# One written-out order of 5935 steps replaced by another in a two-layer graph kernel

## The chip, the cores and the metric

The kernel runs on one core of one Trainium2 chip. The metric is the device time of one execution in microseconds (us). The engines are named as in the profile: PE (TensorE; its weight loads are PEld), DVE (VectorE), ACT (ScalarE), POOL (GpSimd) and SP (SyncE, which here only issues DMAs). Each engine works through its own instructions in program order, and waits at an instruction until what that instruction needs is there.

## The reference, cut to what matters

`x` is 32 batches of 512 channels by 1024 nodes, `adj` is 512 by 512, all in float32.

```
h   = relu(layernorm(x))                        # layer 0, over the 1024 nodes
q   = wq . h ;  k = wk . h                      # one number per node
att = softmax over n of leaky_relu(q[n] + k[m], 0.01)
agg[c, m] = sum over n of h[c, n] * att[m, n]
x   = x + relu(adj @ agg + bm)
h   = relu(layernorm(x))                        # layer 1
x   = x + (adj*adj).T @ h + bias
```

The 1024 x 1024 attention matrix is never formed. A score is linear in `q[n]` on either side of `q[n] + k[m] = 0`, so each output row needs two running sums over the nodes sorted by `q`. The kernel sorts by counting, takes running sums over the sorted rows of `v = adj @ h`, and looks up, for every node, the row of the table where its sign changes.

## The kernel before, in words

`ORDER` (line 35) is one long text, and it is the whole schedule. `names` holds 226 lanes, one for each kind of step and index (`value` 0 to 7, `scan` 0 to 8, and so on); a lane holds that step for each batch in turn. Two base-36 digits give `ahead * 226 + lane`: take from that lane the step that stands `ahead` places from its front (lines 757 to 763). The steps are then issued in that order under `tc.manual_schedule()`, so the text fixes the order of the instructions on every engine and of the DMAs on every queue, and the order in which tiles are taken from the pools.

The steps of a batch, in the order in which they depend on each other:

- `load` (SP, 512 KB each, four), `stats0`, `norm0`, `slopes0`, `relu0` make `h` of layer 0 in place. `stats0` is DVE work for the first six batches and ACT work after.
- `scores` (PE) and a copy on ACT make `q` and `k`; `row` and `columns` bring them into rows and columns; `rank` (DVE, eight) counts each node's place among the `q`; `lower` (ACT, eight) counts the place at which its sign changes; `factors`, `to_rows` and `from_rows` make indices and exponents of them.
- `value` (PE, eight, 8 matmul records each, L474) makes `v` in a PSUM bank, `spread` (ACT, L481) copies it out, `scatter` (POOL, an indirect DMA, L487) writes its rows to a table in DRAM in sorted order.
- `fetch` (SP, three DMAs of 792 KB, L503) reads the table back, `weights` (ACT), `later` (DVE), `totals` (PE) and `stationary` (POOL, L546) make the weights.
- `scan` 0 to 8 (PE, L562; number 4 is L559) makes running sums of 128 rows at a time, one half upwards and one half downwards. Each `scan` has two matmuls, one for each half, and each half needs the last row of the half before it. This carried row is written into the next `vs` rows by `sums`: for batches 5 to 27 ACT copies the sums out (L574), then SP copies one row of 2 KB for each half (L576, L577); for the other batches ACT copies the two rows itself (L572, L573). `sums` then writes the running sums to the table by two DMAs of 132 KB on SP (L580, L581).
- `gather` (POOL, eight indirect DMAs, L586) looks up three table rows for each node, `excess` and `divide` make three factors, `weigh` (ACT, L611) and `combine` (DVE, L615, sixteen) add the rows up. There is one `g` buffer, so the gathers of a batch follow the last `turn` of the batch before.
- `turn0` and `turn1` (PE, L622) transpose the result into a bank; DVE adds it onto `x`, which `reload` (SP, four of 512 KB) has brought again (L626).
- `means`, `stats1` (ACT, four), `norm1`, `slopes1`, `relu1` make `h` of layer 1; `seed` (ACT, L648), `mix` (DVE, L644), `propagate` (PE, 14, L657) and `finish` (DVE, L670 and L674) multiply by `adj*adj` in seven block products instead of eight for batches 0 to 27; the last four batches use `sow`, `plain` (PE, eight, L689) and `close`, with eight. `store` (SP, four of 512 KB, L701) writes the batch out.

There are 8 PSUM banks for all of this, 16 row buffers for `x`, `h` and `mx`, and 5 buffers of three table blocks each for `vs`. Steps of several batches lie between each other: around the scans of batch 14 stand the values of batch 16, the statistics of batch 12 and the products of batch 11. In the order before, the steps from batch 9 to batch 21 repeat: each stretch from a batch's first `scan` to the next batch's is the same 187 steps, shifted by one batch. Before and after that the stretches differ.

Of the kernel before, what the change touches and what calls it, by code (L numbers as in the profile page):

```python
# [33 lines left out]
0a0405002u2w2y30942y01022u96342w352y3630372u30329a332y343a03393b2w382i0y362j2k160w0d090b080c351014  # L34
340m0h0r0u36180n0l0p370o0v120g0q320t330z0k130s3a060f391117353b380e0x192l1i1b0y0j1530942y1c2z371a0i
0w321d331j1e163a2i341g3610071f39353b1h2m2j2k140u18380v120m0h0z132n0r2l110l0n170p0g0o0x0k190q0t0f0y
2w2o2y2x0s2p2u0e3u153v2q1k1i1c0w0j1t1a2m1b1l1d100i161u34141j1h1m18362i3w351f0u371v1g371e3232332j1n
12333a2k0v341w36393b1o0z131x0h0m2l1p112n0l1y0r0g1q170n0x0k1z0f0p1r192v0o310e2w2o30202p1i1c2q0q1s0j
3u150t1a1k0i383v1t0y1b350s1j1e3a371l1g212m162i1f0w1h1u1d39221m2j142k3b25101v3w2338291n1832260u331w
270h0m283a1o242l0v0l1x0z0r0g120n0k130p1p17110f0o2n1y0e0q1q1i1a190y0t0j1z1c2r0i1b0s1r160x2s1j1h2a2d  # L40
562b5c2g1f572i581g5b0w5i551e2e5h2h5e2o5j2c2p2k102f3u592j155k1d205g5a145d1s185f392m2q1k3v3m3r3s0m3q
3o1t3p3t0u210r3b0h1l0n0v121u2l0l0p1m130o3n0z3w1v0g220q252t380k1n230t11290f1w26273e0e1o28170x3g0j24
1x0i3f1p190y3h1j1e2n1y1i1c3c0s3d1q1g3l2m2i1a0w1b1z1f3i1h1r154t3j2k101d2r3k4u2y2s4w2a4v2d41552b5b3z
2g58452e4g3y5h2u2h5d442c4i2f5a16475f3x4m145i40434k185g5k422o314f5e2j462p204n3u562q1k4x4y1s4p1t4950
3v57591l4h5j5148215c4z0h4a1u4b4r4o0l4c522v2x4j1m2w4q2z3m3p1v3w3t3q3r4d1n3n3s1w3o4e22251o4s0u231x2t
4l290g3e26543h1p2l53270v282n0k1y243f0f1q123g0z0e1z0j3c341r3d110i3l3i1j1e360x4t1i1c3j1g3k4u4w303541
1a4v2y4g42131b2r3z2s0m454n3y0r444i171f0n472u4m191h0p4k3x0o43400q464f151d310t4x4y2o4z49202p503u4p2q
0s1s4h2a2m1k51373v4856214a4r322d332b5c4b1t4o574c583a4j395b2v1l2z4q3b2w554d522x1u4e4l381m2g4s532e5i
542i5e3w5d0y5h1v2h1n2j5j2c165k2k2f0w591w5g5a5f1o143m1x3p3o3s3t0m3q1p0r3r3n2n1y1022240n0h280p1q2718
2t0u0l3e261z292l231r0g3g250v123f0k3h0z0f133c0o3d0q0e3l113i1i1c340j1a0x4t3j1b0i3k364u41304v2z4w2x1j  # L50
1g422y2o4g3z2p20451e4n2r3u3y2q3x1s4i402s43171f1935463v4f1h21444p0t4x4y151d1k4m0s50484z2a2m37492d4r
47324h2b332g4a1t563a4k5c4b394o573b2u584c51524j385b1l2e5i2v2h314q2i5e5j2w5k4e555d1u2c2k0y4s2f592j5g
545a5f4d5h161m4l533m3r1v3w3s0m3t3q3p0r3o3n0w220n250p231n0h142910261w2t0l3e273g282l0u240g3f183h1o0k
0v1x3c123d0o0f3l0z3i0e130q4t3j1i1c1p0j3k112n1a1y344u1b4v4w0i413z36452r4g1j1g17423y2s19351h4i444n1f
0x3x4m0t1e400s432a302m2y151d2v2d462b2g4f2u2o5h1q2e2p2h474x3u2c4y1z4z2f2q1k50374p495f5d4855324h331r
4r3a5a4a395i5b204b5g1t4o3b584c5k384j5e4d4q562x571s31592z1l5j52213v5c4e4l1u4k2i4s0y542w51532j1m162k
3m1v3w3p3r3s3o3t3n3q0w22250m230r1n0h29140n10262t1w0l0p273e282l0u240g3g183f1o0k0v1x3h0f123c0o0z3d13
0q0e3l1i1c3i1p0j34111a2n4t1b0i1y3j0x3k2r4u1j1g364w4v1e2s413z303y2z171f44194g351h454m3x420t4i2y4043
0s4n151d2m2f462c2h2u472o4f2e2p2g4x3u1q2b4y2d2q371k504p495h5f1z485d322a4h334a4r3a55395a4b4o3b5i521r
5b384j4c5g20581t5k2i4q5e560y57595j2v5c314k2x2j1s164z512w1l213v2k3m1u3r3p3s3t3q3o4d0m4e0r3n0n0w220p  # L60
250h231m1429102t0l1v3w3e263g4s270g540u183f284l243h0k533c1n0o3d0v120f1w3l3i2l0z0e130q4t3j1i1c113k4u
0j341a1b4w1o174v36410i424g1x1j1f3z3y0x2r4n192s351h1g1p3x300t2y1e452v2x1y0s444i402m151d2a432d2n374m
464f5c56472b324x2g4y2e4z492h502c4p2f4k4a4h33511q572u3a4o48395e5j1z5k4b3b4r58384c5b4j522o5i314d2w4q
2p553u2q2z1r4l591k535a204e5d1t5h5g2i4s5f0y541s162j1l213v2k3m1u3r3s3p3t3q3o3n0w0m22250r230n1m0h2914
100p3w2t1v0l263e273g2l0u280g3f24183h1n0k0v123c1w3d0o0f3l0z3i0e130q4t3j1i1c1o0j3k111a1x344u1b4v4w0i
413z3y361p2r4g441j1g2n1y2s1745191h4m35421f4i3x1e0x0t4n400s2a2m432d302y151d2b462g4f2e5c2h47572c2v4x
2f4y4p49504z4k482o2x4h2p51561q3u374r2q1k5e5j4a1z5k32584b334o3a2u5b4c31394j525i3b551r2w4q2z384d595a
205d1t4e4l5h5g2i4s5f0y54532j1s161l213v2k3m1u3r3s3p3t3q3o3n0m0w220r250n231m0h14290p103w1v2t0l3e263g
272l0u280g3f24183h1n0k0v123c1w3d0o0f3l0z3i0e130q4t3j1i1c1o0j3k111a1x344u1b4v4w0i413z3y361p2r4g441j
1g2n1y2s1745191h4m35421f4i3x1e0x0t4n400s2a2m432d302y151d2b462g4f2e5c2h47572c2v4x2f4y4p49504z4k482o  # L70
2x4h2p51561q3u374r2q1k5e5j4a1z5k32584b334o3a2u5b4c31394j525i3b551r2w4q2z384d595a205d1t4e4l5h5g2i4s
5f0y54532j1s161l213v2k3m1u3r3s3p3t3q3o3n0m0w220r250n231m0h14290p103w1v2t0l3e263g272l0u280g3f24183h
1n0k0v123c1w3d0o0f3l0z3i0e130q4t3j1i1c1o0j3k111a1x344u1b4v4w0i413z3y361p2r4g441j1g2n1y2s1745191h4m
35421f4i3x1e0x0t4n400s2a2m432d302y151d2b462g4f2e5c2h47572c2v4x2f4y4p49504z4k482o2x4h2p51561q3u374r
2q1k5e5j4a1z5k32584b334o3a2u5b4c31394j525i3b551r2w4q2z384d595a205d1t4e4l5h5g2i4s5f0y54532j1s161l21
3v2k3m1u3r3s3p3t3q3o3n0m0w220r250n231m0h14290p103w1v2t0l3e263g272l0u280g3f24183h1n0k0v123c1w3d0o0f
3l0z3i0e130q4t3j1i1c1o0j3k111a1x344u1b4v4w0i413z3y361p2r4g441j1g2n1y2s1745191h4m35421f4i3x1e0x0t4n
400s2a2m432d302y151d2b462g4f2e5c2h47572c2v4x2f4y4p49504z4k482o2x4h2p51561q3u374r2q1k5e5j4a1z5k3258
4b334o3a2u5b4c31394j525i3b551r2w4q2z384d595a205d1t4e4l5h5g2i4s5f0y54532j1s161l213v2k3m1u3r3s3p3t3q
3o3n0m0w220r250n231m0h14290p103w1v2t0l3e263g272l0u280g3f24183h1n0k0v123c1w3d0o0f3l0z3i0e130q4t3j1i  # L80
1c1o0j3k111a1x344u1b4v4w0i413z3y361p2r4g441j1g2n1y2s1745191h4m35421f4i3x1e0x0t4n400s2a2m432d302y15
1d2b462g4f2e5c2h47572c2v4x2f4y4p49504z4k482o2x4h2p51561q3u374r2q1k5e5j4a1z5k32584b334o3a2u5b4c3139
4j525i3b551r2w4q2z384d595a205d1t4e4l5h5g2i4s5f0y54532j1s161l213v2k3m1u3r3s3p3t3q3o3n0m0w220r250n23
1m0h14290p103w1v2t0l3e263g272l0u280g3f24183h1n0k0v123c1w3d0o0f3l0z3i0e130q4t3j1i1c1o0j3k111a1x344u
1b4v4w0i413z3y361p2r4g441j1g2n1y2s1745191h4m35421f4i3x1e0x0t4n400s2a2m432d302y151d2b462g4f2e5c2h47
572c2v4x2f4y4p49504z4k482o2x4h2p51561q3u374r2q1k5e5j4a1z5k32584b334o3a2u5b4c31394j525i3b551r2w4q2z
384d595a205d1t4e4l5h5g2i4s5f0y54532j1s161l213v2k3m1u3r3s3p3t3q3o3n0m0w220r250n231m0h14290p103w1v2t
0l3e263g272l0u280g3f24183h1n0k0v123c1w3d0o0f3l0z3i0e130q4t3j1i1c1o0j3k111a1x344u1b4v4w0i413z3y361p
2r4g441j1g2n1y2s1745191h4m35421f4i3x1e0x0t4n400s2a2m432d302y151d2b462g4f2e5c2h47572c2v4x2f4y4p4950
4z4k482o2x4h2p51561q3u374r2q1k5e5j4a1z5k32584b334o3a2u5b4c31394j525i3b551r2w4q2z384d595a205d1t4e4l  # L90
5h5g2i4s5f0y54532j1s161l213v2k3m1u3r3s3p3t3q3o3n0m0w220r250n231m0h14290p103w1v2t0l3e263g272l0u280g
3f24183h1n0k0v123c1w3d0o0f3l0z3i0e130q4t3j1i1c1o0j3k111a1x344u1b4v4w0i413z3y361p2r4g441j1g2n1y2s17
45191h4m35421f4i3x1e0x0t4n400s2a2m432d302y151d2b462g4f2e5c2h47572c2v4x2f4y4p49504z4k482o2x4h2p5156
1q3u374r2q1k5e5j4a1z5k32584b334o3a2u5b4c31394j525i3b551r2w4q2z384d595a205d1t4e4l5h5g2i4s5f0y54532j
1s161l213v2k3m1u3r3s3p3t3q3o3n0m0w220r250n231m0h14290p103w1v2t0l3e263g272l0u280g3f24183h1n0k0v123c
1w3d0o0f3l0z3i0e130q4t3j1i1c1o0j3k111a1x344u1b4v4w0i413z3y361p2r4g441j1g2n1y2s1745191h4m35421f4i3x
1e0x0t4n400s2a2m432d302y151d2b462g4f2e5c2h47572c2v4x2f4y4p49504z4k482o2x4h2p51561q3u374r2q1k5e5j4a
1z5k32584b334o3a2u5b4c31394j525i3b551r2w4q2z384d595a205d1t4e4l5h5g2i4s5f0y54532j1s161l213v2k3m1u3r
3s3p3t3q3o3n0m0w220r250n231m0h14290p103w1v2t0l3e263g272l0u280g3f24183h1n0k0v123c1w3d0o0f3l0z3i0e13
0q4t3j1i1c1o0j3k111a1x344u1b4v4w0i413z3y361p2r4g441j1g2n1y2s1745191h4m35421f4i3x1e0x0t4n400s2a2m43  # L100
2d302y151d2b462g4f2e5c2h47572c2v4x2f4y4p49504z4k482o2x4h2p51561q3u374r2q1k5e5j4a1z5k32584b334o3a2u
5b4c31394j525i3b551r2w4q2z384d595a205d1t4e4l5h5g2i4s5f0y54532j1s161l213v2k3m1u3r3s3p3t3q3o3n0m0w22
0r250n231m0h14290p103w1v2t0l3e263g272l0u280g3f24183h1n0k0v123c1w3d0o0f3l0z3i0e130q4t3j1i1c1o0j3k11
# [690 lines left out]
```

## Time and profile before

| | |
|---|---|
| runs, us | 2300.36, 2294.92, 2301.21 (median 2300.36) |
| profiled execution, us | 2299.28 |
| its span, us | 2297.6 |
| mean granted TensorE clock | 0.992 |
| PE busy | 2225.3 us (97%) |
| DVE, ACT, POOL busy | 1735.6 (76%), 1703.1 (74%), 704.9 (31%) |
| DMA over the span | 657.77 MB, mean 286 GB/s |

The span is from the first to the last instruction; the 1.7 us between it and the execution's own time lie around it. The page's second part cuts the span into 40 slices of 57 us. A table by windows gives the busy time of each engine in chosen stretches; what a window has over PE's busy time is time in which PE had nothing in work. A matmul that waits for its data behind one that is in work can show as a longer busy time of its line, so a wait can also hide in a busy PE: a line of the timeline then takes longer than the same line elsewhere.

### The profile page before, as it was taken

What the parts mean: (1) busy time and instruction counts of PE and PEld (TensorE: products, weight loads), DVE (VectorE), ACT (ScalarE), POOL (GpSimd) and SP (SyncE); (2) the same over time, 40 slices, a digit from 0 to 9 for tenths busy, and PEclk for the clock granted to TensorE, in tenths of its full rate; (3) what the DMA queues carried; (4) which work ended last, traced back from release to release, by engine and by line L of the source; (5) the groups of instructions that cost most, each with busy time, mean ns of one, the idle gap of its engine ahead of it and who ended that gap; (6) DMA issues with size and microseconds to landing.
All of it is one profiled execution on the core that took longest, in us unless ns stands there. A gap on an engine that the chain in (4) does not pass through costs nothing. (4 is left out here: it accounts for less than half of the span.)

```text
span 2297.6 us, 28803 instructions
## 1 busy us (share of the span) xinstructions
PE 2225.3 (97%) x7344; PEld 954.0 (42%) x7344; DVE 1735.6 (76%) x4876; ACT 1703.1 (74%) x3269; POOL 704.9 (31%) x979
## 2 busy tenths in 40 slices
PE   6999999999999999999999999999999999999987
PEld 3434434344444444444444444444443444444343
DVE  6878878777877877777877877877777878778462
ACT  4698698777677877677877777877777876888752
POOL 2345223233232333232333232333222333234210
PEclk9999999999999999999999999999999999999998
DMA  6697887787888888888888888888888888788951
GB/s 234 225 341 258 310 290 294 276 298 266 314 284 303 299 314 282 291 281 314 295 316 290 300 275 304 309 302 294 300 275 293 301 310 277 283 283 314 368 220 73
DMA packets 217717, 657.77 MB, mean 286 GB/s; under 512 B 39376, under 2 KB 39504, under 8 KB 217552
## 3 DMA queue, kind: packets, MB, share of 16 engines
q1 hardware_dynamic: 153760, 362.16, 45.7%
q0 software_dynamic: 57344, 276.86, 31.4%
q10 hardware_dynamic: 6448, 16.92, 2.6%
q8 instruction: 59, 0.97, 0.2%
q14 instruction: 106, 0.87, 0.1%
HBM read 438.05 MB, written 217.01 MB: 285 GB/s over the span
## 5 line engine op out<-in xcount | busy, mean ns | idle before, releaser
L474 PE MATMUL pv<-wmT,x 128*128 128x512 f32 x2048 | 919.2, 598 | 0.7 <-ACT x L366 0.6
L474 PEld LDWEIGHTS pv<-wmT,x 128*128 128x128 f32 x2048 | 378.5, 190 | 496.5 <-issue 440.2
L487 POOL DMA_INDIRECT td<-v,idx x256 | 261.4, 1021 | 525.6 <-DVE junk L417 218.5
L657 PE MATMUL pg<-h,wsq 128*128 128x512 f32 x896 | 416.5, 599 | 5.2 <-DVE y L674 3.7
L615 DVE SCALAR_TENSOR_TENSOR g<-g,cf 128x512 f32<-128x512 f32 x512 | 365.9, 750 | 9.1 <-ACT g L611 6.5
L586 POOL DMA_INDIRECT g<-td,idg x256 | 245.0, 957 | 275.0 <-DVE y L626 87.2
L562 PE MATMUL sc<-vs,sm 128*64 128x512 f32 x1024 | 298.2, 615 | 18.7 <-DMA vs<-t 11.8
L433 ACT ACTIVATE junk<-qrow,qk 128x1024 uint8<-128x1024 f32 x256 | 293.6, 1147 | 27.7 <-DMA qrow<-qd 24.0
L546 POOL TENSOR_TENSOR sm<-mask_a,wc 128x192 f32<-128x192 f32 x96 | 65.9, 686 | 674.5 <-PE sc L562 445.6
L657 PEld LDWEIGHTS pg<-h,wsq 128*128 128x128 f32 x896 | 165.0, 190 | 236.2 <-issue 183.5
L481 ACT COPY v<-pv 128x512 f32<-128x512 f32 x256 | 145.6, 580 | 142.3 <-PE pv L474 70.3
L574 ACT COPY t<-sc 128x512 f32<-128x512 f32 x288 | 167.3, 581 | 111.3 <-PE sc L562 81.2
L670 DVE SCALAR_TENSOR_TENSOR y<-pg,bm_sb,y 128x512 f32<-128x512 f32 x224 | 166.8, 746 | 95.6 <-PE pg L657 95.5
L657 PE MATMUL pg<-mx,wmix 128*128 128x512 f32 x448 | 213.4, 600 | 1.3 <-ACT pg L648 1.3
L626 DVE SCALAR_TENSOR_TENSOR y<-tr,nbm,y 128x512 f32<-128x512 f32 x256 | 174.9, 746 | 31.7 <-PE tr L622 21.4
L366 ACT ACTIVATE x<-x,nmr,rstd 128x1024 f32<-128x1024 f32 x128 | 150.1, 1232 | 52.2 <-DVE nmr L359 51.6
L422 DVE TENSOR_SCALAR_CACHE_REDUCE junk<-qrow,qk,cnt 128x640 uint8<-128x640 f32 (+6 forms) x224 | 180.4, 805 | 8.2
L337 ACT ACTIVATE junk<-y,nm 128x1024 uint8<-128x1024 f32 x128 | 146.9, 1147 | 31.9 <-DVE nm L345 24.2
L417 DVE TENSOR_SCALAR_CACHE_REDUCE junk<-qrow,qk 128x384 uint8<-128x384 f32 (+6 forms) x224 | 165.8, 740 | 3.6 <-DMA qrow<-qd 1.7
L611 ACT ACTIVATE g<-g,cf 128x512 f32<-128x512 f32 x256 | 165.1, 711 | 4.4 <-DMA qd<-qr 2.2
L366 ACT ACTIVATE h<-y,nmr,rstd 128x1024 f32<-128x1024 f32 x128 | 151.6, 1230 | 4.0 <-DVE nmr L359 2.5
L562 PEld LDWEIGHTS sc<-vs,sm 128*64 128x64 f32 x1024 | 62.3, 135 | 200.7 <-issue 128.7
(135 smaller groups left out, 2535.6 us busy)
## 6 DMA issues: line engine op xcount, KB each, us to landing
vs<-td SPq DMA_DIRECT2D x96, 792.0 KB
td<-t SPq DMA_DIRECT2D x576, 132.0 KB
x<-in_x_dram SPq DMA_DIRECT2D x128, 512.0 KB
y<-in_x_dram SPq DMA_DIRECT2D x128, 512.0 KB
out_dram<-y SPq DMA_DIRECT2D x128, 512.0 KB
qrow<-qd ACTq DMA_DIRECT2D x32, 512.0 KB
vs<-t SPq DMA_DIRECT2D x368, 2.0 KB
td<-v,idx POOLq DMA_INDIRECT x256, 6.2
```

Of the source, the lines that this page charges most:

```text
L366: nc.scalar.activation(h, s.x[c], AF.Relu, bias=s.nmr[:, c : c + 1], scale=s.rstd[:, c : c + 1])
L422: nc.vector.tensor_scalar(junk[:, j * P :], s.qrow[:, j * P :], qc, first, ALU.is_lt, ALU.add, accum_out=s.cnt[:, 1, j : j + 1],)
L433: nc.scalar.activation(junk, s.qrow, AF.Sign, bias=s.qk[:, 1, j : j + 1], accum_out=s.sgn[:, j : j + 1])
L474: nc.tensor.matmul(pv, s.h[c][:, ts(j, P)], wmT[:, c, :], start=(c == 0), stop=(c == NC - 1))
L487: i = nc.gpsimd.indirect_dma_start(tds[s.b % TABLES][:, :], bass.IndirectOffsetOnAxis(ap=s.idx[j // 4][:, j % 4 : j % 4 + 1], axis=0), v[: ...
L562: nc.tensor.matmul(p[ts(k, HP), :], m[:, k, :], s.vs[h][:, 0:C], start=True, stop=True)
L574: nc.scalar.copy(t[:, 0:C], p)
L586: nc.gpsimd.indirect_dma_start(s.g[:, j, :], None, tds[s.b % TABLES].rearrange("(s k) w -> s k w", k=3), bass.IndirectOffsetOnAxis(ap=s.id ...
L615: nc.vector.scalar_tensor_tensor(r, s.g[:, j, k * W : k * W + C], s.cf[:, k, j : j + 1], r, ALU.mult, ALU.add)
L626: nc.vector.scalar_tensor_tensor(xh, pt, nbm[:, o : o + 1], xh, ALU.max, ALU.add, accum_out=s.ys[:, i, o : o + 1])
L657: nc.tensor.matmul(s.pg[key], forms[m][:, r, ts(u, P)], data, start=(m == 2 and r == 0), stop=(r == 1), skip_group_check=True,)
L670: nc.vector.scalar_tensor_tensor(xh, s.pg[key, u], bm_sb[:, c + u : c + u + 1], xh, ALU.add, ALU.add)
```

## The change

Only the text `ORDER` is replaced. The 226 lanes, the functions, the buffers and the number of steps (5935) stay, and each step is issued once, as before. What differs is the place of the steps.

```diff
 ORDER = """
-0a0405002u2w2y30942y01022u96342w352y3630372u30329a332y343a03393b2w382i0y362j2k160w0d090b080c351014
-340m0h0r0u36180n0l0p370o0v120g0q320t330z0k130s3a060f391117353b380e0x192l1i1b0y0j1530942y1c2z371a0i
...
-3q3o3n0m0w220r250n231m0h14290p103w1v2t0l3e263g272l0u280g3f24183h1n0k0v123c1w3d0o0f3l0z3i0e130q4t3j
...
-665w67536452
+2u002w2y01300534943536302u370632333b342w2y0c3830030a373a35392y362w2i040y0w082j2k0z0d340l363233390v
+100i0p380g30173b350k3a2y0o110m142z13fe0t37180u0n0x0f0e0h150r1i1b0q162u12321a2y0y0w2l0j331934962i1j
...
+2r672s5v5m2a652g2c5u532x61565i2z2d5h2e5b2b555731585r5o5e5a592h2f5j68515p5f5k5c5d69635g3m3o3n3t3r54
...
+655154645352
 """
```

Spelled out, the orders begin so (batch after the b, index in brackets):

```
before: pads b0[4], compare_mask, masks, adjacency, load0 b0, load1 b0, load2 b0, load3 b0, load0 b2, load2 b1,
        turn_adjacency, square, load0 b1, load1 b2, stats0 b0[0], load1 b1, stats0 b0[1], ...
after:  load0 b0, adjacency, load1 b0, load2 b0, turn_adjacency, load3 b0, masks, stats0 b0[0], load0 b2,
        stats0 b0[1], stats0 b0[2], load3 b1, load0 b1, stats0 b0[3], pads b0[0], norm0 b0, ...
```

In the new order no stretch repeats: none of the stretches from a batch's first `scan` to the next one's is the same as its neighbour. The steps stay near their old places. On PE, half of the steps move by less than 0.7 us of PE's own work, nine in ten by between 3.1 us earlier and 3.9 us later, and the farthest by 10.7 us earlier and 18.2 us later. On ACT half of the steps move by more than 2 us of ACT's work, on DVE six in ten, on POOL two in three, on SP one DMA in three (a DMA of SP counted at a fixed 0.59 us).

## The prediction

> **What bounds the kernel now.** I read the page's busy times first, then the table by windows, then the list of waits for PE, then two places of the timeline.
>
> ```profile
> PE 2225.3 (97%) x7344; PEld 954.0 (42%) x7344; DVE 1735.6 (76%) x4876; ACT 1703.1 (74%) x3269; POOL 704.9 (31%) x979
> ```
>
> PE has 2225.3 us in work of a span of 2297.6, so all gaps together are 72.3 us, and an order can win no more than these and the waits hidden inside busy matmuls. Where the gaps lie, by windows (span, then PE's busy time):
>
> ```profile
> 0.00:115.00 115.00, 93.23 (x320) 41.42 (x320) 85.80 (x281) 65.15 (x116) 34.06 (x55) 0.96 0.67 229
> 115.00:690.00 575.00, 559.91 (x1887) 234.91 (x1886) 446.51 (x1278) 452.81 (x881) 194.58 (x269) 1.00 0.81 293
> 690.00:1610.00 920.00, 916.63 (x3024) 395.82 (x3024) 716.28 (x2026) 699.64 (x1344) 288.03 (x406) 1.00 0.84 298
> 1610.00:2185.00 575.00, 562.61 (x1870) 239.38 (x1869) 435.32 (x1188) 441.26 (x856) 180.67 (x242) 1.00 0.84 300
> 2185.00:2298.00 113.00, 92.87 (x247) 42.50 (x246) 51.66 (x107) 44.28 (x75) 7.55 (x8) 0.90 0.37 140
> ```
>
> That is 21.8 us at the start, 15.1 in the ramp, 3.4 in the repeating middle, 12.4 behind it and 20.1 in the tail. What ended PE's waits:
>
> ```profile
> PE pp L689 <- ACT pp L685: 13.2, 3, 7.7
> PE sc L562 <- DMA vs<-t: 11.8, 12, 2.3
> PE pt L251 <- DMA adjn<-in_adj_dram: 11.1, 1, 11.1
> PE pq L375 <- ACT x L366: 10.7, 1, 10.7
> ```
>
> The second line is the carried rows. The middle hides more of them. Here is scan 3 of batch 18, and the DMAs of sums 2 that feed it:
>
> ```profile
> 1232.93 1.08 PE L562 MATMUL sc<-vs,sm 128*64 128x512 f32 x4
> 1241.00 2.01 PE L562 MATMUL sc<-vs,sm 128*64 128x512 f32 x4
> ...
> 1235.31 0.53 SPq L576 DMA_DIRECT2D vs<-t  x1
> 1235.89 0.60 SPq L577 DMA_DIRECT2D vs<-t  x1
> ```
>
> The four records take 2.01 us instead of 1.08: the second half waited until about 1241.9, 6.0 us after its row was issued. The rows of sums 6 land 1.3 us after issue (packets of 128 bytes on SP's queue, 16 to a row), those of sums 2 some 5 us, while the gathers run.
>
> Both orders have the same steps. Laid end to end at the smallest start-to-start intervals that the trace shows for each kind and its neighbour (value 3.43 us, product 1.72, scan 0.91, turn 0.44), PE's work is 2153 us before and 2154 after. So the whole question is the waits: 2297.6 - 2153 = 144 us. Below, a distance of two places is the PE work between them in this measure.
>
> **The change part by part.** The sum is against the profiled execution's 2299.28, 1.1 us under the median of the runs.
>
> *Start.* DVE's statistics of batch 0 run without a gap from 12.28 (x0 landed behind 264 + 66 + 1024 + 512 KB) to 17.99, 1.4 each. After, x0 is first on SP and the pads go behind; x1 lands behind 2048 KB, at 234 GB/s 0.8 us later than x0 did, and three statistics remain: 13.1 + 4.2 = 17.3. `scores` starts with the second `relu0` rather than the last. I take -1, ends 0 and -2.5.
>
> *Ramp.* Single waits of 0.3 to 2.3 us make the 15.1; the largest knot is scan 3 of batch 6, with three stores and a load of 512 KB issued on SP from 459.98 to 464.98, ahead of its rows (465.07 and 465.81):
>
> ```profile
> 469.91 1.04 PE L562 MATMUL sc<-vs,sm 128*64 128x512 f32 x2 [0.77 <-DVE junk L422]
> 472.78 1.94 PE L562 MATMUL sc<-vs,sm 128*64 128x512 f32 x2 [1.82 <-DMA vs<-t]
> ```
>
> Idle 0.77 + 1.82, and two records of 1.94 instead of 0.54: 4.0 us behind four transfers. After, one store is left there. Steps on chains (`later`, `slopes0`, `totals`, `weights`) stand 1.6 to 3.5 us of their engine's work earlier on average, fillers (`spread`, `from_rows`, `factors`) 4 to 10 later. I take 6, ends 0 and -12.
>
> *Middle.* The distance from scan 2 to scan 3 stays 7.97 in nearly all batches. But before, 16 of 23 batches had two ACT steps between scan 2 and its `sums` (a spread of 0.58 and a `lower` of 1.34); after, 12 of 23 have none. The copy there started 1.78 us after the scan, elsewhere 1.1; 0.68 less takes most of the 0.93 hidden at 1241. 12 x 0.6 = 7, so -7, ends 0 and -14 (all of the 0.93 in 13 periods, and 1.4 of the 3.4).
>
> *Behind the middle.* 12.4 us, of which 1.8 to 2.4 each at scan 2 of batches 26 and 27: sums 1 stood behind stores waiting for DVE. After, batch 27 has reloads there, which wait for less; batch 26 keeps a store. I take -4, ends 0 and -9.
>
> *Tail.* A chain sets it: the last turn of batch 30 (2200.9), eight gathers, 37 us to the first turn of batch 31 (2238.0), 15 us of statistics and `relu1` to the first `plain` (2262.7).
>
> ```profile
> 2215.73 19.13 PE L689 MATMUL pp<-h,wsq 128*128 128x512 f32 x40 [4.30 <-ACT pp L685]
> 2237.99 1.97 PE L622 MATMUL tr<-ident,g 128*128 128x128 f32 x8 [3.12 <-DVE g L615]
> 2262.73 30.32 PE L689 MATMUL pp<-h,wsq 128*128 128x512 f32 x64 [7.75 <-ACT pp L685]
> ```
>
> After, one `plain` (3.4) moves from before these turns to behind them. The gap at 2238 grows by what the gap at 2262 loses, since the chain is the same. `sow` stands before the last `relu1` instead of behind it: 0.6, and the granted clock falls less after a shorter gap (the first `plain` took 6.2 instead of 3.4 after 7.75 idle). -2, ends +4 and -8.
>
> *Slack.* PE steps with less than 1.9 us of distance to the step that feeds them rise from 68 to 110. Before, 17 products with their seed at 1.3 to 1.9 lost 0.19 each; the few steps under 1.3 lost about 1. 42 x 0.12 = 5, ends 2 (0.05 each) and 17 (0.4 each, half of them at the worse price).
>
> *SP's queue.* Loads and stores of 512 KB that stand within 6 us of PE work before the rows of sums 2 and 3 (batches 5 to 27, the gathers' time) rise from 8 to 36, as the stores leave the place before sums 1, where 8.25 to 17 us of distance made them harmless. 14 stand within 1.1 us. With one store so close, batch 5 lost 0.3 in scan 3. 14 x 0.3 = 4; low end 0; high end 28 x 1.8 = 50 (512 KB at the mean 286 GB/s in front of every row). I take the low value because the copies come earlier in the same place.
>
> The Trainium skill ("DMA: Bandwidth & Descriptors", Queues, rings and completion order) says that a DMA engine works each ring in order and takes turns between rings a packet at a time. By its fit of 436 GB/s the 28 transfers would cost 1.2 each, an estimate of 34 us instead of 4, which would end at 2318. Batch 6, at 1.0 for each transfer, comes near the rule; batch 5, at 0.3, does not.
>
> *POOL.* Two thirds of its steps move by over 2 us, but it is busy 31% and its waits are for PE and DVE; the one use that can bind is gathers behind the last turn. The shortest distance from a `combine` to its turn falls from 6.9 to 1.0 in the middle, and is counted under slack.
>
> Sum: -1 - 6 - 7 - 4 - 2 + 5 + 4 = -11, so 2288.
>
> **Rivals.** *Slower: rows behind stores.* The same gains of 20, but the moved transfers hold the rows up at the price of batch 6, 1.0 for each of 28: 2299.3 - 20 + 28 + 5 for slack = 2312. It decides once the rows lose over 15 us more than before, 0.5 for each. For it: scan 3's distance of 7.97 has nothing left. Against: the earlier copies.
>
> *No change.* Each wait taken away shows the next: the tail is one chain, and scan 3 still ends at 7.97. Gains of 10 (start 1, ramp 3, middle 3, behind it 2, tail 1), costs of 9: 2298.
>
> *Copies too late.* `spread` moves up to 23 us back in ACT's queue, and places in the order with seven or eight PSUM banks taken rise from 51 to 440. If 63 more reuses of a bank within 3 us each wait one copy of 0.58, that is 37: 2288 + 37 = 2325. Before, no wait was seen at such a reuse.
>
> *All goes.* Gains at their ends but the start, 12 + 14 + 9 + 8 = 43, minus 9 and with 1 at the start: 2264.
>
> **How the numbers follow.** Forecast (2270 to 2293) 0.40; all goes (under 2270) 0.10; no change 0.18; rows behind stores 0.22; late copies 0.10. Faster is by more than 0.3%, about what a measurement here can tell from none: under 2293.5. The first two give 0.50. No change is 0.17 within, and 0.01 goes to slower: with the last two 0.33. The range leaves out half of the gains beyond 2264 and part of the two slow cases: 2264 to 2322.
>
> **What would show it.** PE's busy time stays near 2225. Right: the scan line at 1241's place takes near 1.1; `DMA vs<-t` stays under 12 us in PE's waits; the window 115 to 690 has under 10 us of gaps. Wrong: scans of 2 us and more behind a store on SP; PE waits on L481 or L626 for a bank; the gap before the first turn of batch 31 over 7 us without a smaller one at the last products.

## The result and the profile after

| | before | after |
|---|---|---|
| median of 6 runs, us | 2300.4 (2294.84 to 2301.57) | 2277.62 (2274.81 to 2287.55) |
| ratio, 95% interval | | 0.9908 (0.9892 to 0.9924) |
| profiled execution and its span, us | 2299.28, 2297.6 | 2277.74, 2276.0 |

The new order is 0.9% faster, twice the forecast gain: 22.8 us won instead of 11, inside the range (2264 to 2322). The page of the changed kernel, its span and busy times:

```profile
span 2276.0 us, 28735 instructions
...
PE 2218.1 (97%) x7344; PEld 952.9 (42%) x7344; DVE 1753.6 (77%) x4876; ACT 1705.2 (75%) x3269; POOL 711.5 (31%) x979
```

PE does the same work in 7 us less busy time. Those are waits inside busy records, which the gaps do not show. The table by windows of the changed kernel (stretch, its length, then PE's busy time first):

```profile
0.00:115.00 115.00, 99.02 (x331) 43.50 (x332) 90.05 (x289) 65.97 (x121) 33.78 (x54) 0.96 0.70 233
115.00:690.00 575.00, 569.68 (x1927) 242.38 (x1926) 462.10 (x1322) 466.74 (x906) 200.93 (x275) 1.00 0.85 302
690.00:1610.00 920.00, 908.59 (x3022) 391.22 (x3020) 724.91 (x2006) 699.38 (x1343) 288.15 (x401) 1.00 0.84 295
1610.00:2185.00 575.00, 563.11 (x1867) 239.33 (x1867) 438.66 (x1177) 439.51 (x850) 181.12 (x241) 0.99 0.85 297
2185.00:2276.00 91.00, 77.72 (x205) 36.50 (x202) 37.86 (x86) 33.59 (x53) 7.53 (x8) 0.92 0.44 165
```

The gaps are 16.0 at the start (21.8 before), 5.3 in the ramp (15.1), 11.4 in the middle (3.4), 11.9 behind it (12.4) and 13.3 in the tail (20.1). Read alone, the third row says that the middle became 8 us worse. That is not safe to read: the middle of before hides waits in busy records, where the new order shows them as gaps. A measure that counts both is needed. Take PE's work laid end to end as in the prediction (2153 and 2154 us); the time at which PE reaches a step, less the work that stands ahead of that step, is the waiting so far:

| PE reaches | before | after | difference |
|---|---|---|---|
| first scores of batch 0 | 21.8 | 14.8 | -7.0 |
| scan 0 of batch 1 | 28.3 | 24.0 | -4.3 |
| scan 0 of batch 10 | 60.6 | 39.5 | -21.1 |
| scan 0 of batch 18 | 77.5 | 54.2 | -23.3 |
| scan 0 of batch 19 | 79.6 | 62.3 | -17.3 |
| scan 0 of batch 26 | 95.6 | 76.8 | -18.8 |
| scan 0 of batch 31 | 111.4 | 99.2 | -12.2 |
| the end | 144.3 | 121.8 | -22.5 |

In this pair of executions the gain lies in the start and the ramp (21.1) and in the tail (10.3). The batches between win 4 in small sums, lose 6 in batch 18 alone and 7 behind batch 26.

The places hold, but the sizes are those of one pair. The profiles of the versions below have long stretches of either order unchanged, and show how far single executions go. The first scan of batch 9 is reached at 656.0 us in the kernel before, and at 650.8 to 653.2 in three other profiles with the same order up to there. In the changed kernel it is 635.5, and 635.3 to 640.7 in seven others. From the first scan of batch 31 to the end, before takes 138.8 us, and six others with that order 134.2 to 137.1; the changed kernel takes 126.9, and three others 127.9 to 130.0. At both places the profile of before is the slowest of its group, and that of the changed kernel is near the front or at the front, so the table overstates both gains. The timed versions below give 16 for start and ramp and 7 for the tail.

What ended PE's waits after:

```profile
PE sc L562 <- DMA vs<-t: 13.9, 12, 4.0
...
PE tr L622 <- DVE y L696: 3.7, 2, 2.8
PE pp L689 <- ACT pp L685: 3.6, 1, 3.6
PE sc L559 <- ACT vs L573: 3.2, 1, 3.2
```

The wait for the carried rows has grown from 11.8 to 13.9. In the timeline of PE, a scan 3 that no longer waits (batch 12), and scans 2 and 3 of batch 18:

```profile
874.86 1.12 PE L562 MATMUL sc<-vs,sm 128*64 128x512 f32 x4
...
1279.18 1.16 PE L562 MATMUL sc<-vs,sm 128*64 128x512 f32 x4 [1.34 <-DMA vs<-t]
...
1291.40 1.66 PE L562 MATMUL sc<-vs,sm 128*64 128x512 f32 x4 [4.00 <-DMA vs<-t]
```

The first shows what was forecast: 1.12 us, where batch 12 took 1.44 before. Of batches 10 to 22 five are under 1.2 us now, and none was; at the place of the prediction's example (its lines at 1241 are batch 17, not 18) scan 3 still takes 1.66. The other two lines show what was not forecast. The timeline of SP ahead of them says why:

```profile
1270.97 0.73 SPq L581 DMA_DIRECT2D td<-t  x1
1276.51 0.53 SPq L576 DMA_DIRECT2D vs<-t  x1
...
1279.00 0.58 SPq L701 DMA_DIRECT2D out_dram<-y  x1
1279.68 0.39 SPq L309 DMA_DIRECT2D x<-in_x_dram  x1
1280.17 0.89 SPq L701 DMA_DIRECT2D out_dram<-y  x1
1281.15 0.54 SPq L576 DMA_DIRECT2D vs<-t  x1
```

The rows of sums 1 were copied by 1271.4 and issued only at 1276.51. Three transfers of 512 KB stood behind them and so were issued 2.2 to 1.0 us ahead of the rows of sums 2, which landed 9.0 and 9.5 us after issue instead of some 5. What SP waited for, in its list of waits from 1271 to 1277.5:

```profile
SPq L576 <- DMA qrow<-qd: 4.7, 1, 4.7
```

`qrow` (a broadcast of 512 KB for batch 20, issued on ACT at 1269.07, just behind a load and a store) has nothing to do with these rows. But in the built program the DMAs of SP and ACT share eight landing semaphores in rotation, and an issue whose semaphore is still owed by an earlier transfer waits for that one to land.

The tail after, in the timeline of PE:

```profile
2201.59 16.90 PE L689 MATMUL pp<-h,wsq 128*128 128x512 f32 x32 [3.62 <-ACT pp L685]
2221.30 0.90 PE L622 MATMUL tr<-ident,g 128*128 128x128 f32 x3 [2.80 <-DVE y L696]
2223.28 0.47 PE L622 MATMUL tr<-ident,g 128*128 128x128 f32 x1 [1.08 <-DVE g L615]
2224.61 5.33 PE L622 MATMUL tr<-ident,g 128*128 128x128 f32 x28 [0.85 <-DVE y L696]
2229.77 41.37 PE L689 MATMUL pp<-h,wsq 128*128 128x512 f32 x96
```

Where before had gaps of 4.30, 3.12 and 7.75, there are 3.62, then 4.73 in three pieces at the turns of batch 31, and none at all ahead of the last products, which now run on as 96 records without a stop.

### The profile page after: what moved, and what is told of

It reads as the page before. It is cut to its first block, busy times and chain, and to the rows that moved or that the text cites. A ratio compares the mean times of both kernels' runs of the same rounds, so it can differ in the third digit from the quotient of the medians.

```text
span 2276.0 us, 28735 instructions
## 1 busy us (share of the span) xinstructions
PE 2218.1 (97%) x7344; PEld 952.9 (42%) x7344; DVE 1753.6 (77%) x4876; ACT 1705.2 (75%) x3269; POOL 711.5 (31%) x979
## 4 chain that ended last, share of the span: by engine, by line
PE 75%; DMA 9%; DVE 7%; ACT 4%; issue 3%; POOL 1%; SPq 0%; POOLq 0%; ACTq 0%; DVEq 0%
PE pv L474 28%; PE pg L657 27%; PE sc L562 9%; PE pp L689 4%; PE tr L622 4%; DMA vs<-t 3%; PE pq L375 2%; DMA g<-td,idg 2%; DVE g L615 2%; DMA out_dram<-y 1%; DMA td<-t 1%; PE sc L559 1%; DVE y L626 1%; POOL g L586 1%; ACT junk L433 1%
## 5 line engine op out<-in xcount | busy, mean ns | idle before, releaser
L487 POOL DMA_INDIRECT td<-v,idx x256 | 268.7, 1050 | 646.2 <-issue 103.0
L562 PE MATMUL sc<-vs,sm 128*64 128x512 f32 x1024 | 288.9, 618 | 16.2 <-DMA vs<-t 13.9
L626 DVE SCALAR_TENSOR_TENSOR y<-tr,nbm,y 128x512 f32<-128x512 f32 x256 | 177.0, 745 | 45.2 <-PE tr L622 44.3
L422 DVE TENSOR_SCALAR_CACHE_REDUCE junk<-qrow,qk,cnt 128x896 uint8<-128x896 f32 (+6 forms) x224 | 180.4, 805 | 8.2
L546 POOL TENSOR_TENSOR sm<-mask_a,wc 128x192 f32<-128x192 f32 x96 | 60.8, 634 | 393.1 <-DVE wc L523 201.2
L481 ACT COPY v<-pv 128x512 f32<-128x512 f32 x256 | 144.1, 576 | 48.0 <-issue 23.0
L366 ACT ACTIVATE x<-x,nmr,rstd 128x1024 f32<-128x1024 f32 x128 | 152.5, 1234 | 30.9 <-DVE nmr L359 24.0
L611 ACT ACTIVATE g<-g,cf 128x512 f32<-128x512 f32 x256 | 172.2, 713 | 3.3 <-DVE cf L605 2.1
L417 DVE TENSOR_SCALAR_CACHE_REDUCE junk<-qrow,qk 128x128 uint8<-128x128 f32 (+6 forms) x224 | 166.2, 742 | 3.9
L674 DVE TENSOR_TENSOR y<-pg,y 128x512 f32<-128x512 f32 x168 | 114.5, 684 | 69.9 <-PE pg L657 69.0
L366 ACT ACTIVATE h<-y,nmr,rstd 128x1024 f32<-128x1024 f32 x128 | 151.3, 1232 | 12.7 <-DMA out_dram<-y 8.1
```

Source lines behind the costliest of these rows:

```text
L366: nc.scalar.activation(h, s.x[c], AF.Relu, bias=s.nmr[:, c : c + 1], scale=s.rstd[:, c : c + 1])
L422: nc.vector.tensor_scalar(junk[:, j * P :], s.qrow[:, j * P :], qc, first, ALU.is_lt, ALU.add, accum_out=s.cnt[:, 1, j : j + 1],)
L487: i = nc.gpsimd.indirect_dma_start(tds[s.b % TABLES][:, :], bass.IndirectOffsetOnAxis(ap=s.idx[j // 4][:, j % 4 : j % 4 + 1], axis=0), v[: ...
L562: nc.tensor.matmul(p[ts(k, HP), :], m[:, k, :], s.vs[h][:, 0:C], start=True, stop=True)
L611: nc.scalar.mul(r, r, s.cf[:, 0, j : j + 1])
L626: nc.vector.scalar_tensor_tensor(xh, pt, nbm[:, o : o + 1], xh, ALU.max, ALU.add, accum_out=s.ys[:, i, o : o + 1])
```

## The experiments

Every version has the same steps and functions; only the order differs, shown decoded, a step to a line. Each was timed beside runs of the kernel before, whose medians were 2300 to 2307 from one comparison to the next, so ratios are compared, and a gain in us is the ratio's part of 2300. "Waiting" is the measure of the table above.

### Start and ramp

```diff
 (all steps up to the first scan of batch 10)
-old order
+new order
 (the rest) old order
```

> The new order up to the first scan of batch 10, the old order of the remaining steps from there. Theory A (start and ramp hold nearly all of the gain: in the profile of the changed kernel PE reaches the first scan of batch 10 with 21 us less waiting than before, 7 of them by the first scores): 2300 - 21 = 2279, as fast as the changed kernel, with 18 us or more won at that scan. Theory B (the terms of the prediction, 1 for the start and 6 for the ramp): 2293. Theory C (what the ramp wins is given back at the next wait of the repeating middle): 2300, with the lead at batch 10 shrinking to nothing by batch 18.

Ratio 0.9953 (0.9936 to 0.9971), 11 us won. The lead at scan 0 of batch 10 is 18.0 as A has it, but directly behind the cut PE stands 6.3 us at a product of batch 7 that waits for a `finish` of DVE, and at batch 11 the lead is 9.0. It is 7.8 at batch 18 and 6.6 at the end, so C falls; the 9 went at one place, which the cut may have made. The next version cuts where only two steps differ between the two.

```diff
-(all steps up to the first scan of batch 10) new order
+(all steps up to the 1881st, ahead of scan 2 of batch 10) new order
 (the rest) old order
```

> The new order up to the place ahead of scan 2 of batch 10 where the two orders have nearly the same steps behind them (two differ), the old order from there. The first cut of this kind, at the first scan of batch 10, won 18 us there and lost 9 directly behind the cut. Theory A (start and ramp win 20, and the old middle, having nothing to catch up, keeps it): 2301 - 20 = 2281, with no gap of over 2 us behind the cut. Theory B (the 9 are not the cut's: what the ramp wins is in part given back at the first full period of the old middle): 2290. Prediction's terms: 2293.

Ratio 0.9929 (0.9912 to 0.9945), 16 us won; the waiting at scan 0 of batch 11 is 45.8 against 62.9, a lead of 17.1, of batch 19 it is 16.4, and at the end 15.3. A is nearer than B or the prediction's terms: the old middle keeps most of what the ramp won, and the 9 were the first cut's.

```diff
+load0 b0
+adjacency
-pads b0[4]
-compare_mask
-masks
-adjacency
-load0 b0
 load1 b0
 ... (the new order to its step 154, then the old one)
```

> Only the first 154 steps in the new order (the first load ahead of the pads, statistics, scores and values of batch 0), the old order from there. Theory A (the scores 7 us earlier, and 4 of them kept): 2301 - 4 = 2297, up to 7 if nothing catches up. Theory B (prediction: three statistics behind a first load 0.8 later, -1): 2300. In the profile: first scores at 18.4 (A) or 24 (B) instead of 25.4.

Ratio 0.9975 (0.9964 to 0.9987), 6 us won, nearer to A. The scores begin at 18.47 as in the new order. In the timeline of DVE, the kernel before (statistics of batch 0, and the second instruction of `slopes0`):

```profile
12.28 1.29 DVE L324 BATCH_NORM_STATS2 st<-x 128x6 f32<-128x512 f32 x2 [9.34 <-DMA x<-in_x_dram]
...
18.79 1.13 DVE L356 SCALAR_TENSOR_TENSOR step<-step,rstd 128x4 f32<-128x4 f32 x1
```

and the same of the changed kernel:

```profile
4.73 1.29 DVE L324 BATCH_NORM_STATS2 st<-x 128x6 f32<-128x512 f32 x2 [2.38 <-DMA x<-in_x_dram]
...
10.31 1.29 DVE L324 BATCH_NORM_STATS2 st<-x 128x6 f32<-128x512 f32 x2 [4.05 <-DMA x<-in_x_dram]
...
15.43 0.16 DVE L356 SCALAR_TENSOR_TENSOR step<-step,rstd 128x4 f32<-128x4 f32 x1
```

The second load lands at 10.31, where the prediction had 13.1. It stands behind as much as x0 did before and 182 KB more, but SP begins 1.0 us sooner (the pads waited for DVE), and the bytes go faster: 2048 KB in 9.5 us from the first issue, against 1866 KB in 10.5. Five profiles with the old start have x0 at 11.8 to 12.3, nine with the new one x1 at 10.1 to 10.4. What slows the bytes is not shown. The pads' own rows move at 262 GB/s (from 3 to 4 us) and are over by 4.4; the slow stretch lies behind them, with 90 and 94 GB/s from 4 to 6 us, against 75 and 225 in the changed kernel. And the second and third instructions of `slopes0` take 0.16 each instead of 1.13 and 0.54.

### The middle

```diff
 (up to the first scan of batch 10) old order
 (to the first scan of batch 26)
-old order
+new order
 (the rest) old order
```

> The old order up to the first scan of batch 10, the new one to the first scan of batch 26, the old one behind it. Theory A (the waits counted on the two profiles): the middle wins 2 to 3 us up to batch 17 and loses 6 at batch 18, so 2302 (+2). Theory B (the prediction's terms for the middle: 7 won by the copies of sums 2, 2 to 3 lost to slack, 3 to the rows): 2298 (-2). Either way no large part of the gain of 23 lies here; a time under 2292 would refute both.

Ratio 1.0031 (1.0017 to 1.0046): 7 us lost (4 to 11), nearer to A; no gain lies here as a whole, and the loss is more than the 2.3 us by which the waiting of the first pair grows from batch 10 to 26. The waiting rises by 9.4 from batch 18 to 19, so the knot of batch 18 comes with this piece of the order. What the pieces are worth was tried in the old middle, where each period is alike:

```diff
 scan b15 (2)
+sums b15 (2)
 rank b17 (3)
 spread b17 (2)
 ...
 lower b17 (3)
 value b17 (6)
-sums b15 (2)
```

> The old order with one thing changed: in batches 8 to 23 the copies and rows of sums 2 stand directly behind scan 2, ahead of a spread and a lower on ACT (16 batches). By the prediction's term (0.6 for each, out of the 0.93 hidden at scan 3): 16 x 0.6 = 10, so 2291, and the scan 3 records fall from 2.0 to 1.1 to 1.4. Rival (the spread and the lower that now stand behind are waited for instead, or the row's landing and not the copy decides): 2298 to 2301.

Ratio 0.9968 (0.9958 to 0.9977), 7.4 us won, 0.46 for each of 16 batches instead of 0.6. The mechanism holds: the copy starts 1.15 instead of 1.78 us after scan 2 begins, and the loss at scan 3 falls from 0.92 to 0.36 in each of batches 10 to 22, while scan 4 loses 0.15 more.

```diff
 sums b15 (0)
-store b12 (3)
-store b12 (2)
 ...
 sums b15 (1)
+store b12 (3)
+store b12 (2)
 ...
 sums b15 (2)
```

> The old order with the two stores between sums 0 and sums 1 moved directly ahead of the rows of sums 2, in batches 9 to 22 (28 transfers of 512 KB). Prediction's price, 0.3 for each: 2301 + 8 = 2309. Rival of the rows behind stores, 1.0 for each: 2329. By 436 GB/s, the fit that the Trainium skill gives (an estimate, DMA: Bandwidth & Descriptors), 1.2 for each would be 2335. Theory of two clean batches (with one store so close the rows of the new order landed as late as with none, 4.2 to 5.8): under 2305.

Ratio 0.9976 (0.9965 to 0.9986): 5.5 us won, where the prediction's price gave 8 lost and the rival's 28. Both are wrong in sign; only "under 2305" holds. SP in the timeline of this version:

```profile
1084.19 0.59 SPq L581 DMA_DIRECT2D td<-t  x1
1084.88 1.03 SPq L701 DMA_DIRECT2D out_dram<-y  x2
1090.83 0.54 SPq L576 DMA_DIRECT2D vs<-t  x1
```

and PE at its scan 3:

```profile
1096.57 1.41 PE L562 MATMUL sc<-vs,sm 128*64 128x512 f32 x4
```

In the queue the two stores stand directly ahead of the rows of sums 2, but in time they are issued 6 us ahead, when SP has nothing else to do. The second row of sums 2 lands 5.01 us after issue instead of 5.34 (batches 10 to 22), the loss at scan 3 is 0.65 instead of 0.92, and the rows of sums 1, no longer behind the stores, follow their copy after 1.02 instead of 1.50. The first gather of the batch before is issued 5.3 instead of 3.9 us ahead of the rows; that this is what speeds them in this version is only argued. Over nine profiles and batches 8 to 27, the second row of sums 2 landed after 5.28 us with no load or store of 512 KB issued within 7 us ahead (53 cases), after 5.19 with two at 2.5 to 7 us (76), after 1.8 to 8.4 with two within 2.5 us (7), and after 9.5 and 9.6 with three within 2.5 us (2, both batch 18 of the new order). The seven are of two kinds. Four are batch 25, where the first gather is issued over 3 us behind the rows, and land after 1.8 to 2.3 us. Three are batch 26 of the new order, where it is issued some 3 us ahead of them, and land after 7.8 to 8.4. So transfers directly ahead delayed the rows much only where the gathers ran too.

The Trainium skill ("DMA: Bandwidth & Descriptors", Queues, rings and completion order) has each ring worked in order, and by its fit of 436 GB/s (Anatomy of one DMA — SWDGE (gpsimd) path) this version was to lose 34, an estimate. The runs do not contradict the order; they show that two transfers issued 6 us ahead are out of the way by then.

Batch 6 of the old order, from which the prediction took its price of 1.0 for each transfer, shows the same. Six profiles (the kernel before and five versions) have the old order around it, and in each the rows of sums 2 are issued with the same four transfers 0.5 to 5.3 us ahead. In three of them the first gather is issued 0.5 to 0.9 us behind the first row, the second row lands late, and scan 3 loses 3 us or more. In the kernel before, where the first row is issued at 465.07, POOL has it at:

```profile
465.99 1.00 POOL L586 DMA_INDIRECT g<-td,idg  x1 [3.01 <-PE tr L622]
```

In the other three it is issued 2.2 to 2.9 us behind, and scan 3 waits for nothing. The version with the moved stores is one of them (first row on SP, first gather on POOL, scan 3 of batch 6 on PE):

```profile
464.82 0.69 SPq L576 DMA_DIRECT2D vs<-t  x1
...
467.68 1.00 POOL L586 DMA_INDIRECT g<-td,idg  x1 [4.64 <-PE tr L622]
...
470.76 1.08 PE L562 MATMUL sc<-vs,sm 128*64 128x512 f32 x4
```

So the largest knot of the ramp was there in half of the executions with the same steps around it, and the four transfers alone did not make it.

### The knots of the new order

```diff
 sums b18 (1)
-store b15 (0)
-load0 b21
-store b15 (2)
 ...
 sums b18 (3)
+store b15 (0)
+load0 b21
+store b15 (2)
 (likewise a load and a store of batch 26; and one late store:)
+store b26 (1)
 reload2 b28
 ...
-store b26 (1)
```

> The new order with six DMA issues of SP moved: in batches 18 and 26 the stores and the load that stand between sums 1 and sums 2 go behind sums 3, and one late store of batch 26 goes ahead of the reloads of batch 28, so that the second relu1 of batch 28 finds its buffer free. Theory A (two or three transfers of 512 KB directly ahead of the rows cost 4 to 6 us there, and the late store 3 to 4): rows of sums 2 land in 6 us or less instead of 9.5 and 8.4, the gaps of 4.0, 2.8 and 3.2 us at scan 3 of batches 18 and 26 and scan 4 of batch 30 go, and the time is 2278 - 11 = 2267. Theory B (the waits move to the next rows, those of sums 3 and 4, which now stand ahead of the transfers): 2278 within 3.

Ratio 0.9902 (0.9882 to 0.9922), no faster than the changed kernel: B, though by another way than it says. Scan 3 of batch 18 loses its wait (rows landed after 4.6 and 5.2 us), and then scan 5 pays. Its line in the timeline of PE (`ORDER` is 23 lines shorter here, so L539 is L562):

```profile
1307.89 2.32 PE L539 MATMUL sc<-vs,sm 128*64 128x512 f32 x4 [2.78 <-DMA vs<-t]
```

and from ACT's waits between 1298 and 1307 (L343 is L366, a `relu1`):

```profile
ACT h L343 <- DMA out_dram<-y: 7.1, 1, 7.1
```

ACT, which works in order, stood 7.1 us until a store had given a row buffer free, and the copy of sums 4 stood behind it. In batch 26 it stood 6.2 us at the statistics of the postponed load. A transfer has a due time at both ends; to postpone it moves the wait to whoever uses its buffer. The late store was a gain at its place: the wait at scan 4 of batch 30 (3.21) is gone.

```diff
-load1 b21
 scores b20
-store b15 (3)
 row b20
 ...
 sums b18 (1)
+load1 b21
+store b15 (3)
 (and the late store of batch 26 as above)
```

> The new order with one load and one store of batch 18 moved on SP from ahead of the broadcast of qrow (of batch 20) to behind the rows of sums 1, and the late store of batch 26 ahead of the reloads of batch 28. Theory A (SP stood 4.7 us at the rows of sums 1 until qrow had landed, since they share one of eight landing semaphores, and this made the three transfers behind them late): qrow lands 2 us or more sooner after its issue than 7.4, the rows of sums 1 are issued within 1 us of their copy instead of 5.1, scan 3 waits less than 2 us instead of 4.0, scan 4 of batch 30 not at all instead of 3.2: 2278 - 8 = 2270. Theory B (rows behind five transfers instead of three land later still, whatever SP does): scan 3 waits 5 us or more, 2275 to 2280.

In its place A holds. `qrow` landed 3.6 us after its issue instead of 7.4, and the rows of sums 1 are issued 0.8 us after their copy began instead of 5.7. SP in the timeline:

```profile
1281.30 0.83 SPq L576 DMA_DIRECT2D vs<-t  x1
...
1284.16 0.55 SPq L309 DMA_DIRECT2D x<-in_x_dram  x1
1284.81 0.87 SPq L701 DMA_DIRECT2D out_dram<-y  x2
1285.77 1.09 SPq L309 DMA_DIRECT2D x<-in_x_dram  x1
1286.95 1.45 SPq L701 DMA_DIRECT2D out_dram<-y  x1
1289.19 0.54 SPq L576 DMA_DIRECT2D vs<-t  x1
```

and PE at scan 3:

```profile
1296.48 1.42 PE L562 MATMUL sc<-vs,sm 128*64 128x512 f32 x4 [0.91 <-issue]
```

Five transfers, 5.0 to 2.2 us ahead, delayed the rows to 6.2 us; three, 2.2 to 1.0 ahead, to 9.0. Batch 18 costs 3.1 instead of 8.1, batch 30 2.3 instead of 7.7. The version makes two changes to SP's wait at once (less in front of `qrow`, and another semaphore for the rows), and does not tell them apart. In the whole time nothing of the 10 us is seen: ratio 0.9913 (0.9896 to 0.9929), where A expected 0.987. The profile waits 9.6 us more than that of the changed kernel by the first scan of batch 18, in a stretch where the order is the same, and 3 more in the tail. Whether the knots belong to the order, and not to one execution, the same order again shows:

```diff
 (the changed kernel, nothing edited)
```

> The changed kernel once more, on the same chip as the version above. If the places where it lost on its first profile are the order's and not that execution's, scan 3 of batch 18 waits 3 us or more again and scan 4 of batch 30 2 us or more, and the ratio to the kernel before is 0.989 to 0.992. If they were that execution's, they are not there and others are.

Ratio 0.9917 (0.9898 to 0.9936). Both knots are back, in PE's timeline:

```profile
1299.55 2.43 PE L562 MATMUL sc<-vs,sm 128*64 128x512 f32 x4 [4.86 <-DMA vs<-t]
...
2126.84 1.38 PE L559 MATMUL sc<-vs,sm 128*128 128x512 f32 x2 [2.41 <-ACT vs L573]
```

They belong to the order. (This run was timed beside the last version below, which is "the version above" of its text; the kernel before took 2307 there, and 2300 beside the first execution.) But this execution, batch 18 left out, waits 11 us more from batch 10 to 26 than the first one of the same order (40.7 against 29.2). Between executions that differ by so much, 10 us of repair at two places did not show in a ratio whose interval is some 8 us wide; whether they are given back elsewhere stays open.

### The tail

```diff
 (up to scan 5 of batch 30) old order
-old order
+new order
```

> The old order up to scan 5 of batch 30, the new one from there, so only the tail is new. Theory A (waits counted on the two profiles: 10 us less from the first scan of batch 31 to the end): 2290. Theory B (the prediction: one chain, the gap before the last products wanders to the first turn of batch 31): 2298. The gaps of 4.3, 3.1 and 7.8 us before the products of batch 30, the first turn and the first product of batch 31 tell them apart: under A they sum to under 9, under B to over 12.

Ratio 0.9969 (0.9956 to 0.9982), 7 us won, nearer to A. The gaps are 3.62 ahead of a product, 4.78 at the turns of batch 31 and none ahead of its first product; with one more of 0.37, 8.8.

### The parts put together

```diff
 (up to the cut ahead of scan 2 of batch 10) new order
 (old middle, each period:)
 weights b15
+later b15
 finish b12 (2, 0)
 ...
-later b15
 (sums 2 and stores as in the two versions above)
 (from scan 5 of batch 30) new order
```

> The new order up to the cut ahead of scan 2 of batch 10, the old repeating middle with three regular changes (sums 2 directly behind scan 2 in batches up to 23, the two stores behind the rows of sums 1 instead of ahead of them up to batch 27, `later` directly behind `weights` on DVE up to batch 24), and the new order from scan 5 of batch 30. Theory A (the parts add up: ramp 16, sums 2 6, stores 6, tail 7 by the runs so far, and 0.46 hidden in each scan 0 of the old middle, 15 x 0.46 = 7): 2300 - 42 = 2258. Theory B (the middle's gains show the next wait and half of their 19 goes): 2268. Theory C (the parts were worth something only in their own surroundings): 2278 or more, no better than the new order as a whole.

Ratio 0.9829 (0.9808 to 0.9850), 39 us won, between A and B, nearer to A. The move of `later` has a reason that the prediction did not see. POOL in the timeline of the kernel before, ahead of scan 0 of batch 15:

```profile
1069.57 0.50 POOL L546 TENSOR_TENSOR sm<-mask_b,wc 128x192 f32<-128x192 f32 x1
```

and that scan on PE:

```profile
1069.66 1.54 PE L562 MATMUL sc<-vs,sm 128*64 128x512 f32 x4
```

The second half of the scan waits until POOL has made its weights at 1070.07, and the four records take 1.54 instead of 1.08. In the versions that leave `later` in place scan 0 loses 0.46 to 0.51 in each of batches 10 to 22. Here, the same scan on PE:

```profile
1050.92 1.11 PE L562 MATMUL sc<-vs,sm 128*64 128x512 f32 x4
```

The loss is gone. Scan 3 loses 0.15 instead of 0.92, and scan 4, the next in line, 0.42 instead of 0.03. So the last version has sums 3 closer too:

```diff
 scan b15 (3)
+sums b15 (3)
 ...
 spread b17 (0)
 norm1 b13 (1)
-sums b15 (3)
 (and a store and a reload of batch 25 to behind the rows of sums 1)
```

> The version put together from the parts (ratio to the kernel before 0.9829), with two more changes: in batches 10 to 24 sums 3 stand directly behind scan 3, ahead of a spread and a norm1 on ACT, because scan 4 now loses 0.42 in each period; and in batch 25 a store and a reload go from ahead of the rows of sums 1 to behind them, so that these rows no longer need the landing semaphore that the 4 KB transfer qd still owes (3.6 us on SP, and 3.2 at scan 2). Theory A: 15 x 0.35 + 3 = 8 less, ratio 0.980. Theory B (the loss at scan 4 wanders on to scan 5 or to the products that use the later spread): ratio 0.9825 to 0.984.

Ratio 0.9818 (0.9803 to 0.9834), 42 us won, the fastest version; 2264.4 against 2288.0 for the changed order beside it. From the ratio alone the last step cannot be told from none. In the profile scan 4 loses 0.16 instead of 0.42, but scan 3 0.28 instead of 0.15 and one product (7, 1) 0.26 instead of 0.01, as B has it. The waiting from batch 25 to 26 falls from 6.9 to 1.7. That cannot be put down to the freed semaphore alone: the version also has sums 2 of batches 24 to 27, with the stores ahead of them, directly behind scan 2, which its text does not name. Its page:

```profile
span 2258.9 us, 28723 instructions
...
PE 2207.3 (98%) x7344; PEld 948.1 (42%) x7344; DVE 1737.3 (77%) x4876; ACT 1697.5 (75%) x3269; POOL 702.1 (31%) x979
```

## Why the prediction was right or wrong

The sign was right and the time lay in the range, but the gain was twice the forecast, and the terms were wrong in both directions: the ends of the order won more than was forecast and the middle lost 7 where it was to lose 2, so 2278 lies near 2288 partly by luck. The waiting gives each term for the first pair of profiles, the timed versions give the larger pieces:

| term of the sum | forecast | by the waiting, one pair | timed by itself |
|---|---|---|---|
| start | -1 (0 to -2.5) | -4.3 | -6 (-3 to -8) |
| ramp, to batch 10 | -6 (0 to -12) | -16.8 | with the start -16 (-13 to -20) |
| middle, to batch 26: sums 2, slack, SP's queue | -7, +5, +4 | +2.3 | +7 (+4 to +11) |
| behind the middle, to batch 31 | -4 (0 to -9) | +6.6 | not tried |
| tail | -2 (+4 to -8) | -10.3 | -7 (-4 to -10) |
| sum | -11 | -22.5 | -21 (-17 to -25), the whole order |

The timed pieces sum to -16; where the other 5 lie is open.

- **Start.** Mis-sized, outside its ends. The step "at 234 GB/s 0.8 us later than x0 did" failed: x1 landed 2.0 us sooner than x0 had (10.31 against 12.28). SP began 1.0 sooner, and the bytes went faster for a reason that is not shown. The scores came 7.0 sooner, of which 2.7 went again by batch 1. Alone it won 6 (3 to 8).
- **Ramp.** Mis-sized, but not clearly outside its ends: the 16.8 belongs to one pair of executions, and start and ramp together won 16 by time, the start alone 6, which leaves some 10. The end of 12 came from the 15.1 us of gaps; the hidden waits were left out, though the reading of scan 3 had just shown that they exist. The largest knot was misread. Batch 6, from scan 2 to the products behind scan 3, had lost 7.3 in that execution, not the 4.0 that I counted from two gaps and one long record; but in three of six profiles with the same four transfers its scan 3 lost nothing, so "4.0 us behind four transfers" is no price of the order.
- **Middle.** The step "0.68 less takes most of the 0.93" was right: alone it gave 0.46 a batch. (The example at 1241 is batch 17.) In the changed kernel scan 3 lost 0.78 a batch in batches 10 to 22 instead of 0.92, and without batch 18 only some 0.43. The *POOL* paragraph failed, which put nothing down for it: scan 0 waited for POOL in nearly every period, hidden, and its 0.51 fell to 0.03, 6 us that no term had. Scans 2, 4 and 5 lost some 0.6 more a batch together, 7.8 us over 13 batches with batch 18's share in it, where slack had 5. Timed, the middle lost 7 where the terms summed to 2.
- **SP's queue.** "14 x 0.3 = 4" is wrong in sign: 28 transfers moved to the same place in the queue won 5.5. The count by PE work was the error. What matters is the time of issue and whether the gathers run then; stores with free buffers are issued at once, 5 us and more ahead. The cost is in the knots where SP was held: batch 18 (6) and batch 26.
- **Behind the middle.** The gain of 4 did not come. Batch 26 kept its knot (8.2 against 5.1 to the next batch; a load and a store 1.9 and 1.5 us ahead of the rows), and batch 30 lost 4 that I had not looked for: a store of batch 26 stood on SP behind the table writes of batch 30 until 2100, landed 11 us later, and a `relu1` needed its buffer. The 6.6 itself is not steady: this stretch took 340.0 us in the first profile of the order and 333.6 in the second, with 330.1 to 334.2 in the six profiles that have the old order there (and 3 us less of PE's work in it).
- **Tail.** "The gap at 2238 grows by what the gap at 2262 loses, since the chain is the same" failed: the chain became shorter. From the last turn of batch 30 to the first of batch 31 it took 33.6 us instead of 36.9, from the last turn to the first product of batch 31 13.6 instead of 14.6, and four products of batch 30 filled that stretch instead of two, so that the gap there went and the last eight products took 27.6 instead of 30.3 (34.5, 13.6 and 27.6 in the version with the new tail alone). The gap at the turns is 4.7 instead of 3.1, and 3.7 of it is turns that wait for a `close` (L696). A smaller step failed too, that the clock falls less after a shorter gap: the first product took 6.6 us after 3.62 idle here, against 5.4 after 4.30 and 6.3 after 7.75 before. Alone the tail won 7, near the lower end of -8.
- **Rivals.** Rows behind stores: refuted as a price for every transfer, true in two batches; the price itself came from batch 6, which does not bear it. No change: refuted. Copies too late: among PE's waits none is for L481 or L626, against the 37 of that rival; 3.7 us at two turns are for a `close`, and the second profile of the order has 1.5 at a turn for L626. (Before had 2.6 for L626, so waits of this kind were there to be seen.) "All goes" had the direction, but at 2264 it was farther off than the forecast.
- **What would show it.** Of the signs for right one came: under 10 us of gaps in the ramp (5.3). The scan at 1241's place takes 1.66, not near 1.1, and `DMA vs<-t` is 13.9, not under 12, although the kernel is faster. A sign for wrong came in batch 26, where scan 3 takes 2.37 us behind a store on SP. PE's busy time fell by 7 instead of staying, since it had hidden waits. No gap is left ahead of the last products.

## What to carry to other kernels

Judge an order by time minus work laid end to end, at chosen steps, and not by gaps alone: in the old middle all gaps were 3.4 us, and moving sums 2 won 7.4, mostly out of waits inside busy records. Do not size a piece from one pair of profiles: here the pair said 21 for start and ramp and 2 lost in the middle, the timed versions 16 and 7. A transfer ahead of a small urgent row cost by when it was issued and by whether the gathers ran then, not by its place in the queue, and what holds the issuing queue may be the landing of an unrelated transfer. Where one period repeats, moving the same few steps in each repetition (a copy, two stores, one small DVE step) did more than an irregular order: from batch 10 to 26 the last version waits 24 us, the new order 37 and 50 in its two profiles, the old one 35 to 41 in three.

## What was not expected of the hardware

- A transfer of SP waits for the landing of a transfer that it does not depend on, because eight landing semaphores go round among the DMAs of SP and ACT. Before, SP stood 21.8 us in 16 waits of the carried rows' second half for a `reload`; after, 2.1. These are lines of SP's waits, before and after:

```profile
SPq L577 <- DMA y<-in_x_dram: 21.8, 16, 2.4
```

```profile
SPq L577 <- DMA y<-in_x_dram: 2.1, 2, 1.6
```

- The 4 KB of `qd`, on ACT's own queue, held SP for up to 3.6 us in batch 25 of the version put together, with four transfers of 512 KB just issued: a small transfer on another queue is not quick for that.
- The first 1866 KB took 10.5 us with the pads in front, the first 2048 KB 9.5 without them. The pads' rows of 2.1 KB are not slow in themselves (262 GB/s); the loads behind them ran at 90 and 94 GB/s for 2 us. The reason stays open.
- The same four transfers directly ahead of a row delayed it in three executions and not in three others, with the issue of the first gather (0.5 to 0.9 or 2.2 to 2.9 us behind the row) as the difference that the profiles show.
- The same order, profiled twice, reached the first scan of batch 26 with 76.8 and 94.6 us of waiting, and the medians of the kernel before differ by 7 us between comparisons. Differences under about 5 us were read from single places, not from totals, and the totals of one pair were off by about as much.
